# A graph attention layer on one core: more row loads on ACT, a new order of SP's loads at the end

## The chip, the cores and the metric

The kernel runs on one core of one Trainium2 chip. The core has five engines with a queue of their own: PE (matrix products), DVE and ACT (vector and scalar work), POOL (here: it issues gathers), and SP (it only issues transfers). The metric is device time in microseconds (us), the median of several runs.

## The reference

12,500 nodes with 128 features each, and 412,500 edges sorted by destination, each with 64 features. One layer of graph attention with 4 heads of 32:

```python
h = jnp.maximum(_layernorm(x, axis=-1), 0.0)
h = (h @ W_node.T).reshape(num_nodes, H, HD)
e = (edge_features @ W_edge.T).reshape(num_edges, H, HD)
att = jnp.sum(jnp.concatenate([h[src], h[tgt], e], axis=-1) * a, axis=-1)
att = jnp.where(att > 0, att, 0.2 * att)
m = jnp.maximum(segment_max(att, tgt), 0.0)
ex = jnp.exp(att - m[tgt])
denom = segment_sum(ex, tgt) + (num_edges - deg)[:, None] * jnp.exp(-m)
out = x + segment_sum((ex / denom[tgt])[:, :, None] * h[src], tgt)
```

So for every edge one row of `h` has to be fetched by its source, weighted, and added to the row of its destination.

## The kernel before

A first stage computes a table in the chip's memory: one row of 144 floats (576 bytes) per node, with the four heads of `h`, ones for the sums, and each node's parts of the logits. A second small table, `near`, holds the destinations' part.

The edges are then cut into 461 chunks of 896, that is 7 tiles of 128 edges each; 7 chunks make a batch, 49 tiles, and there are 66 batches, 0 to 65 (the last has 6 chunks). A loop written out by hand runs over them. In iteration b:

- POOL issues the gathers of batch b+1 (`gather`, L648). One gather fetches the 128 rows of one tile. Ahead of a batch's gathers stands a small memset (`gate`, L643) that waits until the scatter of batch b-2 is done, since the rows' buffers `hs` form a ring of three.
- One or two tiles of a batch are not gathered but fetched row by row (`by_row`): SP and ACT each issue single loads of 576 bytes at addresses that they first read into registers, up to 32 at once (`row_by_row`, L670 the addresses, L674 the loads). `act_rows(b)` is how many of a batch's rows ACT issues; SP issues the rest. ACT issues batch b+2's rows in iteration b, in pieces: `MIDDLE` behind the copy of `spread`, `WHILE` behind a merge that has an output part after it, the rest at the iteration's end (`act_some`). SP issues rows of batch b+1: up to `FRONT` of them before the node logits of batch b+1, and the rest behind, at least `SPROWS` an iteration, the surplus going to batch b+2.
- SP also loads the node logits of batch b+1 from `near` into the one buffer `lw` (`load_near`, L590), which must wait until the choice of batch b has read it; the edge features `eft` (L582); and `pen_sb` (L696).
- DVE and ACT weigh batch b (`weigh`, `weigh_part`): DVE waits for the batch's rows (L689), adds the logits (L765), runs two scans (L775, L777); ACT takes the exponentials (L780); DVE multiplies the rows (L831), and PE scatters them into sums by destination (L838).
- ACT copies `lw` for batch b+1 (`spread`, L603), DVE chooses from it by predicated copies (`choose`, L607 to L620) and marks the destinations (`mark`, L733).
- Every second iteration, and in each of the last ones, DVE merges the sums of the batches into the accumulator `acc` (`merge`). It reads the columns' numbers into registers (`columns`, L865) after the copy of `here` (L899) and before the multiplication of L902, which waits for ACT's two exponentials (L895, L896).
- When enough is merged, a part of the output is finished (`finish`): the output of 98 tiles is made in 15 parts, 13 of 7 tiles and the last two of 4 and 3. ACT takes L992, DVE L994 to L999, PE 32 products (L1006), DVE adds in two steps (L1011), and SP stores.

In the last iterations the order differs: in iteration 64 batch 65 is chosen and marked before batch 64 is weighed, and batch 65 is weighed in two parts, the first over four of its seven rows of tiles.

The sizes that the change touches:

```python
FRONT = 64
ACTROWS = 112
MIDDLE = 16
WHILE = 32
EVERY = 4
```

Of the kernel before, what the change touches and what calls it, by code (L numbers as in the profile page):

```python
# [16 lines left out]
ENG = mybir.EngineType  # L17
# [6 lines left out]
H = 4  # L24
# [7 lines left out]
CB = 2 * SB - 1  # L32
NBT = -(-NCH // CB)
# [6 lines left out]
W = 32  # L40
# [3 lines left out]
NB = -(-N // P)  # L44
NQ = NB * (P // W)
GB = 7
XB = 9
LOOSE = 1
# [17 lines left out]
RL = 32  # L66
SPROWS = 112
FRONT = 64
ACTROWS = 112
MIDDLE = 16  # L70
WHILE = 32
EVERY = 4
HEADROWS = 32
EPS = 1e-5

# [15 lines left out]

def by_row(b):

    return (1 if b % EVERY == 0 or b == LOOSE + 1 else 2) if LOOSE < b < NBT else 0


def act_rows(b):

    return 0 if b <= LOOSE + 1 else MIDDLE if b == NBT - 1 else ACTROWS


def merges():
# [15 lines left out]
def parts():  # L118


    got, b0 = [], 0
    for n in [GB] * (NB // GB - 1) + [GB - GB // 2, GB // 2]:
        last = (b0 + n) * P + 2 * W
        b = next((b for _, b in merges() if chunk_of(b + 1) * CE * N >= last * E), NBT - 1)
        got.append((b0, n, b if b0 + n < NB else NBT - 1))
        b0 += n
    return got
# [11 lines left out]
def kernel(  # L139
# [12 lines left out]
    nc = tc.nc  # L152
# [87 lines left out]
    with (  # L240
# [275 lines left out]
        k = -2  # L516
# [146 lines left out]
    def row_by_row(s, engine, kind, n):  # L663

        last = s.left
        s.left = max(0, last - n)
        some = last - s.left
        while last > s.left:
            first = max(s.left, last - RL, (last - 1) // P * P)
            _, at = nc.values_load_multi_w_load_instructions(  # L670
                row_at[s.b - 2:s.b - 1, first:last], engines=[kind], min_val=0, max_val=(NB * P - 1) * WIDE,
                skip_runtime_bounds_check_because="a src is below N, and N at most NB * P")
            for i, v in enumerate(at, first):
                by_itself(engine.dma_start(s.hs[i % P:i % P + 1, i // P, :].bitcast(U8),  # L674
                                           table_b[ds(v, WIDE)].rearrange("(o c) -> o c", o=1)),
                          f"lone{s.b}", lone_sems, lone_done, s.b % ROWSEMS)
            last = first
        return n - some
# [184 lines left out]
    def columns(c, k):  # L863

        _, got = nc.values_load_multi_w_load_instructions(  # L865
            q0[0:1, c:c + k], engines=[ENG.DVE], min_val=0, max_val=NQ - 2,
            skip_runtime_bounds_check_because="a dst is at most N, so its column is at most N // W")
        return got

    def merge(c0, count, r, breaks=None):  # L870

        n = count if breaks is None else 2 * count
        step = n // count
        breaks = new[:, c0:c0 + n] if breaks is None else breaks.rearrange("p c k -> p (c k)")
        flat = (AW - 1) * (n + 1)
        ended = c0 + count == NCH
        up = ps.tile([P, BANKS * 512], F32, name="up")
        f = up[:, :flat].rearrange("p (d c) -> p d c", d=AW - 1)
        nc.vector.memset(f[:, :, 0], 0.0)
        m = r[:, AW - 1, 1:n + 1]  # L880
        run = work.tile([P, MC + 1], F32, name="run")
        nc.vector.tensor_copy(run[:, 0:1], carry_m)
        mc = work.tile([P, MC], F32, name="mc")
        nc.vector.tensor_scalar(mc[:, :n], m, 0.0, None, op0=OP.max)
        nc.vector.tensor_tensor_scan(run[:, 1:n + 1], breaks, mc[:, :n], run[:, 0:1],
                                     op0=OP.add, op1=OP.max)
        if not ended:
            nc.vector.tensor_copy(carry_m, run[:, n:n + 1])
        dif = work.tile([P, 2, MC], F32, name="dif")
        nc.vector.tensor_tensor(dif[:, 1, :n], m, run[:, 1:n + 1], op=OP.subtract)  # L890
        nc.vector.tensor_tensor(dif[:, 0, :n], run[:, 0:n], run[:, 1:n + 1], op=OP.subtract)
        nc.vector.tensor_tensor(dif[:, 0, :n], dif[:, 0, :n], breaks, op=OP.add)
        nc.vector.tensor_scalar(f[:, HD + 1, 1:n + 1], breaks, 1.0 / BIG, 1.0, op0=OP.mult, op1=OP.add)
        scale = up[:, 512:512 + MC]
        nc.scalar.activation(scale[:, :n], dif[:, 1, :n], AF.Exp)  # L895
        nc.scalar.activation(f[:, :HD + 1, 1:n + 1], dif[:, 0, None, :n].to_broadcast([P, HD + 1, n]), AF.Exp)  # L896
        nc.vector.tensor_copy(r[:, :AW - 1, 0], carry)
        here = here_ps[:, :count, :]
        nc.vector.tensor_copy(here, lastm[:, c0:c0 + count, :])  # L899
        got = columns(c0, min(CB, count))  # L900
        part = r[:, :HD + 1, 1:n + 1]
        nc.vector.tensor_tensor(part, part, scale[:, None, :n].to_broadcast([P, HD + 1, n]), op=OP.mult)  # L902
        val = work.tile([P, CE], F32, name="up")[:, :flat].rearrange("p (d c) -> p d c", d=AW - 1)
        nc.vector.tensor_tensor_scan(val.rearrange("p d c -> p (d c)"), f.rearrange("p d c -> p (d c)"),
                                     r[:, :AW - 1, :].rearrange("p d c -> p (d c)"), 0.0,
                                     op0=OP.mult, op1=OP.add)
        if not ended:
            nc.vector.tensor_copy(carry, val[:, :, n])
        put = up[:, :MC * 2 * AW].rearrange("p (c j d) -> p c j d", c=MC, j=2)
        nc.vector.tensor_tensor(put[:, :count, :, AW - 1], here,  # L910
                                run[:, step:n + 1:step, None].to_broadcast([P, count, 2]), op=OP.mult)
        for k in range(2):
            nc.vector.tensor_tensor(put[:, :count, k, :AW - 1], val[:, :, step:n + 1:step].rearrange("p d c -> p c d"),
                                    here[:, :, k:k + 1].to_broadcast([P, count, AW - 1]), op=OP.mult)
        for i0 in range(0, count, CB):
            if i0:
                got = columns(c0 + i0, min(CB, count - i0))
            for i, v in enumerate(got):
                cols = acc[:, ds(v, 2), :]
                nc.vector.tensor_tensor(cols, cols, put[:, i0 + i, :, :], op=OP.add)  # L920
# [62 lines left out]
    def finish(pool, psum, tag, em, b0, n):  # L983

        q = slice(b0 * 4, (b0 + n) * 4)
        full = min(n, (N - b0 * P) // P)
        left = N - (b0 + full) * P
        xg = held_x.pop(b0, None)
        if xg is None:
            xg = load_part(pool, b0, n)  # L990
        em = em[:, :n * 4]
        nc.scalar.activation(em, acc[:, q, AW - 1], AF.Exp, scale=-1.0)  # L992
        rest = pool.tile([P, GB * 4], F32, name="rest")[:, :n * 4]
        nc.vector.tensor_scalar(rest, acc[:, q, HD + 1], -1.0, float(E), op0=OP.mult, op1=OP.add)  # L994
        nc.vector.tensor_tensor(em, em, rest, op=OP.mult)
        nc.vector.tensor_tensor(em, em, acc[:, q, HD], op=OP.add)
        nc.vector.reciprocal(em, em)
        wgt = pool.tile([P, BUF], F32, name="a")[:, :GB * 4 * HD].rearrange("p (q d) -> p q d", d=HD)
        nc.vector.tensor_tensor(wgt[:, :n * 4, :], acc[:, q, :HD], em[:, :, None].to_broadcast([P, n * 4, HD]),  # L999
                                op=OP.mult)  # L1000
        w4 = wgt.rearrange("p (b s) d -> p b s d", s=4)

        po = psum.tile([P, 2, 512], F32, name=tag)[:, :, :2 * GB * HD].rearrange("p k (h b d) -> p k h b d", h=2, d=HD)
        for h in range(H):
            for s in range(4):
                nc.tensor.matmul(po[s * W:(s + 1) * W, h // 2, h % 2, :n, :],  # L1006
                                 ident[:, h * W:(h + 1) * W], w4[:, :n, s, :], start=True, stop=True,
                                 tile_position=(0, s * W))
        for k in range(2):
            cols = xg[:, :n, k * 2 * HD:(k + 1) * 2 * HD].rearrange("p b (h d) -> p h b d", d=HD)  # L1010
            nc.vector.tensor_tensor(cols, po[:, k, :, :n, :], cols, op=OP.add)  # L1011

        def store():
            nc.sync.dma_start(out[b0 * P:(b0 + full) * P, :].rearrange("(b p) d -> p b d", p=P), xg[:, :full, :])
            if full < n:
                nc.scalar.dma_start(out[(b0 + full) * P:N, :], xg[:left, full, :])

        return store
# [76 lines left out]
    with tc.manual_schedule():  # L1095
# [17 lines left out]
        for b in range(NBT - 1):  # L1113
# [5 lines left out]
                batch(b + 3).ends = index(b + 3)  # L1119
            front = 0  # L1120
            if b:
                front = FRONT - row_by_row(batch(b + 1), nc.sync, ENG.SP, FRONT if b < NBT - 2 else FRONT // 2)
            load_near(batch(b + 1))
            if before and merge_of(b - 1)[1] == b - 1:
                for b0, n, behind in parts():
# [332 lines left out]
```

## Time and profile before

| | |
|---|---|
| median of 3 runs | 3956.34 us (3948.43 to 3957.4) |
| the profiled execution | 3947.4 us |
| its span, from the first to the last instruction | 3945.6 us |
| busy: POOL, DVE, PE, ACT | 75%, 62%, 28%, 11% |
| gathers issued by POOL (L648) | 3045 |
| row loads issued by SP, by ACT (L674) | 7248, 6960 |
| granted TensorE clock, mean | 0.603 |

Busy time counts an engine's own work; what a queue does to issue a transfer isn't counted, except that POOL's gathers are. In rows of the profile SPq and ACTq are the queues of SP and ACT, "x32" is a count of instructions merged into one row, and "[0.30 <-issue]" is idle time before an instruction and what ended it; "issue" means that no wait shows.

### The profile page before, as it was taken

The page shows a single profiled execution, that of the slowest core. Times are in us where ns is not written, and L with a number is a line of the kernel's source. Part 1 is how long each engine was busy: PE and PEld are TensorE (multiplying, and loading weights), DVE is VectorE, ACT ScalarE, POOL GpSimd, SP SyncE. Part 2 cuts the span into 40 slices and gives each one's busy share as a digit, 9 for nine tenths or more (in the row PEclk, how much of TensorE's full clock was granted, in tenths as well). Part 3 has the DMA queues.
Part 4 walks back from the last instruction along what each step waited for, and adds up shares of the span by engine and source line. Part 5 has one row for each costly group of instructions (what it writes and reads, how often), then busy time and mean ns, then how long its engine had stood idle before and what let it go on. Part 6 is the DMA issues. An engine that isn't in the chain of part 4 may idle for free.

```text
span 3945.6 us, 96319 instructions
## 1 busy us (share of the span) xinstructions
PE 1111.9 (28%) x27848; PEld 636.6 (16%) x27848; DVE 2452.5 (62%) x4384; ACT 433.4 (11%) x693; POOL 2952.7 (75%) x3188
## 2 busy tenths in 40 slices
PE   5532233223222232222222222232232222222231
PEld 4321011111111111111111111111111111011011
DVE  7766576556566566465566565566566566556577
ACT  5220011100110011011011010011011011011010
POOL 7777777777777777777777777777777777777773
PEclk9766666555665665565655665655555565656665
DMA  7444444444444444434444444434434434444431
GB/s 222 135 111 122 102 116 112 116 94 133 97 117 115 95 113 122 110 90 117 102 102 115 105 104 115 115 89 122 110 95 117 110 93 112 114 96 115 115 94 48
DMA packets 294926, 436.70 MB, mean 111 GB/s; under 512 B 84002, under 2 KB 207454, under 8 KB 294386
## 3 DMA queue, kind: packets, MB, share of 16 engines
q0 software_dynamic: 99584, 229.07, 26.0%
q1 hardware_dynamic: 167376, 189.90, 15.5%
q10 hardware_dynamic: 27426, 11.50, 1.3%
q8 instruction: 220, 3.60, 0.4%
q14 instruction: 320, 2.62, 0.2%
HBM read 414.67 MB, written 15.51 MB: 109 GB/s over the span
## 4 chain that ended last, share of the span: by engine, by line
POOL 48%; issue 20%; DVE 8%; SPq 7%; ACTq 7%; DMA 2%; PE 1%; ACT 1%; DVEq 0%; POOLq 0%
POOL hs L648 48%; ACTq L674 6%; SPq L674 5%; DVE hs L831 2%; DVE pick L620 1%; SPq L670 1%; ACTq L670 1%; DMA hs<-table,ends 1%; DMA lw<-near 1%; SPq L590 1%; DVE hot L733 1%; PE pa L838 0%; DVE up L775 0%; PE up L1006 0%; DVE m L777 0%
## 5 line engine op out<-in xcount | busy, mean ns | idle before, releaser
L648 POOL DMA_INDIRECT hs<-table,ends x3045 | 2880.0, 946 | 924.1 <-issue 921.6
L838 PE MATMUL pa<-hs,hot 128*32 128x35 f32 x25480 | 483.5, 243 | 2532.5 <-DVE hs L831 2164.3
L838 PEld LDWEIGHTS pa<-hs,hot 128*32 128x32 f32 x25480 | 426.6, 149 | 2625.1 <-issue 2533.2
L765 DVE TENSOR_TENSOR logits<-hs,pick 128x196 f32<-128x196 f32 x65 | 32.4, 498 | 878.6 <-DVEq L689 877.3
L714 PE MATMUL z<-eft,wa 128*32 128x512 f32 (+3 forms) x1056 | 493.0, 607 | 20.5 <-DMA eft<-in_ef 17.0
L831 DVE TENSOR_TENSOR hs<-hs,exr 128x924 f32<-128x924 f32 (+2 forms) x466 | 478.5, 1097 | 0.0
L780 ACT ACTIVATE both<-a 32x224 f32<-32x224 f32 (+2 forms) x268 | 103.2, 385 | 2801.3 <-DVE a L778 2067.3
L620 DVE COPY_PREDICATED pick<-exr,lw 128x3136 f32<-128x3136 int32 x65 | 237.5, 3654 | 11.5 <-ACT pick L603 9.8
L620 DVE COPY_PREDICATED pick<-exr,pick 128x1568 f32<-128x1568 int32 (+2 forms) x195 | 227.2, 1165 | 6.7
L603 ACT COPY pick<-lw 128x3136 f32<-128x3136 f32 x65 | 182.2, 2803 | 105.1 <-ACTq L689 88.6
L714 PEld LDWEIGHTS z<-eft,wa 128*32 128x32 f32 (+1 forms) x1056 | 106.9, 120 | 370.6 <-issue 359.3
L786 DVE STREAM_TRANSPOSE exr<-both 128x224 f32<-128x224 f32 (+1 forms) x67 | 28.3, 423 | 214.4 <-ACT both L780 212.7
L775 DVE TENSOR_TENSOR_SCAN up<-pen_sb,z 32x896 f32<-32x896 f32 (+1 forms) x67 | 133.3, 1990 | 34.7 <-DMA pen_sb<-pens 32.5
L920 DVE TENSOR_TENSOR acc<-acc,up 128x70 f32 x461 | 105.1, 228 | 67.2 <-issue 51.3
L777 DVE TENSOR_TENSOR_SCAN m<-pen_sb,up 32x896 f32<-32x896 f32 (+1 forms) x67 | 132.6, 1979 | 2.3
L733 DVE TENSOR_TENSOR hot<-exr,key 128x448 f32<-128x448 f32 (+1 forms) x260 | 128.9, 558 | 5.8
L770 DVE TENSOR_TENSOR up<-z,zst 32x224 f32<-32x224 f32 (+2 forms) x268 | 103.3, 385 | 13.0 <-PE z L714 0.2
L784 DVE SCALAR_TENSOR_TENSOR both<-pen_sb,up 32x224 f32<-32x224 f32 (+2 forms) x268 | 100.0, 373 | 3.8
L1006 PE MATMUL up<-a,ident 128*32 128x224 f32 (+2 forms) x480 | 44.5, 546 | 187.7 <-DVE a L999 187.7
L252 POOL DMA_INDIRECT hs<-in_x,ends x67 | 63.5, 948 | 20.4 <-issue 19.5
L774 DVE TENSOR_TENSOR z<-up,a 32x896 f32<-32x896 f32 (+1 forms) x67 | 72.0, 1075 | 2.3
L778 DVE TENSOR_TENSOR a<-z,m 32x896 f32<-32x896 f32 (+1 forms) x67 | 71.4, 1066 | 2.3
(192 smaller groups left out, 1102.6 us busy)
## 6 DMA issues: line engine op xcount, KB each, us to landing
eft<-in_ef SPq DMA_DIRECT2D x66, 1792.0 KB
hs<-table SPq DMA_DIRECT2D x7248, 0.6 KB
hs<-table ACTq DMA_DIRECT2D x6960, 0.6 KB
hs<-table,ends POOLq DMA_INDIRECT x3045
lw<-near SPq DMA_DIRECT2D x461, 64.0 KB
pen_sb<-pens SPq DMA_DIRECT2D x66, 98.1 KB
table<-rows ACTq DMA_DIRECT2D x9, 648.0 KB
xg<-in_x SPq DMA_DIRECT2D x13, 448.0 KB
```

The costliest lines, as they stand in the source:

```text
L603: nc.scalar.copy(s.pick[:, :, :s.chunks, :], lw[:, None, :s.chunks, :n].to_broadcast([P, T, s.chunks, n]))
L620: nc.vector.copy_predicated(s.pick[:, :, :s.chunks, :n], bit[:, :, :, None].to_broadcast([P, T, s.chunks, n]), more)
L648: load = nc.gpsimd.indirect_dma_start(out=s.hs[:n, t * CB + q, :], out_offset=None, in_=table[:, :], in_offset=bass.IndirectOffsetOnAxis(a ...
L674: by_itself(engine.dma_start(s.hs[i % P:i % P + 1, i // P, :].bitcast(U8), table_b[ds(v, WIDE)].rearrange("(o c) -> o c", o=1)), f"lone{s. ...
L714: s.made = own_half(s, nc.tensor.matmul(s.z[:, part], wa3[:n, j, :], s.eft[:n, j, part], start=(j == 0), stop=(j == SB - 1)))
L733: nc.vector.tensor_tensor(s.hot[:, :, q0:q0 + n, :].rearrange("p t q r -> p q t r"), rows_ps[:, None, None, :].to_broadcast([P, n, T, W]), ...
L770: on_half(s, nc.vector.tensor_tensor(grouped(up, g), grouped(s.z, g), zst[g * R:(g + 1) * R, t0:t1, :], op=OP.add))
L775: on_half(s, nc.vector.tensor_tensor_scan(up[:, e0:e1], s.pen[:, e0:e1], z, 0.0, op0=OP.add, op1=OP.max))
L777: nc.vector.tensor_tensor_scan(mp[:, ::-1], s.pen[:, e1:e0:-1], up[:, e0:e1][:, ::-1], 0.0, op0=OP.add, op1=OP.max)
L831: nc.vector.tensor_tensor(rows, rows, ex_ps[:, t0:t1, q * H:(q + 1) * H, None].to_broadcast([P, t1 - t0, H, HB]), op=OP.mult)
L838: scattered[s.b] = nc.tensor.matmul(pa[h * W:(h + 1) * W, q * AW:(q + 1) * AW], s.hot[:, t, q, :], s.hs[:, t * CB + q, h * AW:(h + 1) * AW ...
L920: nc.vector.tensor_tensor(cols, cols, put[:, i0 + i, :, :], op=OP.add)
```

## The change

ACT issues 128 rows of a batch instead of 112, and only one batch in eight (not in four) has a single tile by rows, so 118 tiles come by rows instead of 111. The last batch has one tile by rows (before: two), all by SP; of batch 64's rows ACT issues 80. In iterations 63 and 64 SP issues 96 and 48 rows ahead of the node logits (before: up to 64 and 32). The column numbers of a merge are loaded at its head. An output part's products are issued by halves, with DVE's addition of a half behind each. Of the last two output parts the first now has 3 tiles and the second 4.

```diff
-ACTROWS = 112
+ACTROWS = 128
-EVERY = 4
+EVERY = 8
 def by_row(b):
-    return (1 if b % EVERY == 0 or b == LOOSE + 1 else 2) if LOOSE < b < NBT else 0
+    if b in (LOOSE + 1, NBT - 1):
+        return 1
+    return (1 if b % EVERY == EVERY // 2 else 2) if LOOSE < b < NBT else 0
 def act_rows(b):
-    return 0 if b <= LOOSE + 1 else MIDDLE if b == NBT - 1 else ACTROWS
+    return 0 if b <= LOOSE + 1 or b == NBT - 1 else MIDDLE + 2 * WHILE if b == NBT - 2 else ACTROWS
 def parts():
-    for n in [GB] * (NB // GB - 1) + [GB - GB // 2, GB // 2]:
+    for n in [GB] * (NB // GB - 1) + [GB // 2, GB - GB // 2]:
 def merge(c0, count, r, breaks=None):
         breaks = new[:, c0:c0 + n] if breaks is None else breaks.rearrange("p c k -> p (c k)")
+        got = columns(c0, min(CB, count))
...
         nc.vector.tensor_copy(here, lastm[:, c0:c0 + count, :])
-        got = columns(c0, min(CB, count))
 def finish(pool, psum, tag, em, b0, n):
-        for h in range(H):
-            for s in range(4):
-                nc.tensor.matmul(po[s * W:(s + 1) * W, h // 2, h % 2, :n, :],
-                                 ident[:, h * W:(h + 1) * W], w4[:, :n, s, :], start=True, stop=True,
-                                 tile_position=(0, s * W))
         for k in range(2):
+            for h in (2 * k, 2 * k + 1):
+                for s in range(4):
+                    nc.tensor.matmul(po[s * W:(s + 1) * W, k, h % 2, :n, :],
+                                     ident[:, h * W:(h + 1) * W], w4[:, :n, s, :], start=True, stop=True,
+                                     tile_position=(0, s * W))
             cols = xg[:, :n, k * 2 * HD:(k + 1) * 2 * HD].rearrange("p b (h d) -> p h b d", d=HD)
             nc.vector.tensor_tensor(cols, po[:, k, :, :n, :], cols, op=OP.add)
 # the loop over batches
-                front = FRONT - row_by_row(batch(b + 1), nc.sync, ENG.SP, FRONT if b < NBT - 2 else FRONT // 2)
+                front = FRONT - row_by_row(batch(b + 1), nc.sync, ENG.SP, (MIDDLE + WHILE if b == NBT - 2 else FRONT + WHILE if b == NBT - 3 else FRONT))
```

## The prediction

> **What bounds the kernel now.** I read the page first, for the busy engine and the chain that ended last, then the waits, then the timeline of ACT, SP and POOL in three places: just after the start, in the middle, at the end.
>
> ```profile
> PE 1111.9 (28%) x27848; PEld 636.6 (16%) x27848; DVE 2452.5 (62%) x4384; ACT 433.4 (11%) x693; POOL 2952.7 (75%) x3188
> DMA  7444444444444444434444444434434434444431
> POOL 48%; issue 20%; DVE 8%; SPq 7%; ACTq 7%; DMA 2%; PE 1%; ACT 1%; DVEq 0%; POOLq 0%
> L648 POOL DMA_INDIRECT hs<-table,ends x3045 | 2880.0, 946 | 924.1 <-issue 921.6
> ```
>
> POOL issues 3045 gathers, 946 ns busy each and then 0.30 us in which it waits for nothing the profile shows: (2880.0 + 924.1) / 3045 = 1.249 us a gather, 3804 of the 3945.6 us. A batch has 49 tiles, of which 1 or 2 come row by row; 47 gathers are 58.7 us. So a tile taken off POOL is worth 1.249 us, as long as the rest keeps up. The waits show who keeps up:
>
> ```profile
> ACT both L780 <- DVE a L778: 2067.3, 48, 59.2
> ACT both L780 <- issue: 677.5, 17, 46.8
> SPq L590 <- DVE pick L620: 272.7, 20, 26.9
> DVE r L902 <- ACT up L896: 46.0, 34, 7.5
> DVE xg L1011 <- PE up L1006: 45.8, 14, 3.4
> ```
>
> The exponentials of L780 come once a batch, and behind them stand the multiplication and the scatter. In 48 cases ACT waited for DVE: there it had time to spare. In 17 it was released by "issue": DVE was ready and ACT's queue was still issuing row loads. ACT's 11% busy says nothing of this, for a row load is not counted as busy.
>
> **Step 1, POOL.** Tiles by rows go from 111 to 118: batches 8, 16, ... 64 get a second tile (8 gathers fewer), batch 65 loses one (1 more). 7 × 1.249 = 8.7 us off POOL's stream; 10.0 us off before batch 65's gathers begin.
>
> **Step 2, ACT issues 16 rows more a batch.** Does it fit? The middle of the run, ACT's timeline:
>
> ```profile
> 1506.34 1.58 ACT L780 ACTIVATE both<-a 32x224 f32<-32x224 f32 x4 [55.36 <-DVE a L778]
> 1523.04 10.53 ACTq L674 DMA_DIRECT2D hs<-table  x32
> 1535.06 26.09 ACTq L674 DMA_DIRECT2D hs<-table  x64
> 1563.90 1.59 ACT L780 ACTIVATE both<-a 32x224 f32<-32x224 f32 x4 [30.06 <-DVE a L778]
> 1623.71 1.59 ACT L780 ACTIVATE both<-a 32x224 f32<-32x224 f32 x4 [55.12 <-DVE a L778]
> 1640.05 37.70 ACTq L674 DMA_DIRECT2D hs<-table  x96
> 1683.26 1.59 ACT L780 ACTIVATE both<-a 32x224 f32<-32x224 f32 x4 [44.98 <-DVE a L778]
> 1685.60 45.77 ACTq L674 DMA_DIRECT2D hs<-table  x111
> 1741.72 1.59 ACT L780 ACTIVATE both<-a 32x224 f32<-32x224 f32 x4 [53.78 <-DVE a L778]
> ```
>
> From the exponentials to its last row ACT needs 54.8 us in a batch with a merge and an output part (1506.34 to 1561.15), 54.0 in one with a merge, 48.1 without: 102.5 us for two batches. Sixteen more rows cost 5.3 us by the 32 rows in 10.53 (which hold no load of offsets), 6.6 by the 111 in 45.77 (which hold four), 6.3 by the 96 in 37.70; I take 6.3, since the new pieces need about as many loads a row. That makes 115.1 us a pair, with 0.2 us between last row and next exponentials 115.3; the ends are 113.3 and 115.9. POOL's pair becomes 94.25 gathers and two gates, 117.9 us. ACT still fits, with 2.6 us to spare where it had 15. Where a merge batch has only 2.7 us free (1561.15 to 1563.90) the next exponentials come some 4 us late; the batch after it, with 10 us free, takes that up.
>
> But the run does not start level:
>
> ```profile
> 245.90 0.11 POOL L643 MEMSET gate<- 128x1 f32 x1
> 292.75 0.25 PE L838 MATMUL pa<-hs,hot 128*32 128x35 f32 x1
> 305.86 0.11 POOL L643 MEMSET gate<- 128x1 f32 x1
> 328.93 1.58 ACT L780 ACTIVATE both<-a 32x224 f32<-32x224 f32 x4 [39.77 <-issue]
> 1547.88 0.11 POOL L643 MEMSET gate<- 128x1 f32 x1
> ```
>
> The memset before each batch's gathers marks when the batch before it is issued. Batch 25 is issued at 1547.88 and has its exponentials at 1563.90, 16 us later; batch 3 is issued at 245.90 and has them at 328.93, 83 us later. ACT and DVE start 67 us behind POOL and have caught up by the middle. After the change this backlog is 67 + 2 × 6.3 = 80 us at batch 3 and shrinks by 2.6 us a pair instead of 15: 80 / 2.6 = 31 pairs, batch 65. It is used up only just before the end. On the way POOL itself must not stall: it may overwrite a buffer when the scatter of three batches before is done, 293.00 for the gate at 305.86, 12.9 us free. One batch of 6.3 us leaves 6.6. After that the room grew by 15 us a pair and now grows by 2.6, so it stays near 7 us for long. I cost a stall at nothing; if it comes, it is the few us by which 7 is exceeded, once.
>
> **Step 3, the end.** SP's order sets when batch 65's node logits (`lw`) are there.
>
> ```profile
> 1544.95 3.35 SPq L590 DMA_DIRECT2D lw<-near  x7
> 1550.19 18.22 SPq L674 DMA_DIRECT2D hs<-table  x48
> 1573.74 23.55 SPq L674 DMA_DIRECT2D hs<-table  x64
> 1598.71 3.50 SPq L590 DMA_DIRECT2D lw<-near  x7
> 1652.26 3.28 SPq L590 DMA_DIRECT2D lw<-near  x7
> 1658.40 36.00 SPq L674 DMA_DIRECT2D hs<-table  x96
> 1698.23 17.37 SPq L674 DMA_DIRECT2D hs<-table  x48
> 1717.00 3.34 SPq L590 DMA_DIRECT2D lw<-near  x7
> 3553.79 3.22 SPq L590 DMA_DIRECT2D lw<-near  x7
> ```
>
> From one load of node logits to the next SP needs 53.8 us with 112 rows between (1544.95 to 1598.71), 64.7 with 144. The line through both gives 59.2 for 128, 70.2 for 160, 48.3 for 96; simple proportion to 64.7 gives 57.5, 71.9 and 43.2. Batch 60's load (3553.79) waits for the choice of batch 59, not for SP, so it moves with POOL to 3545. By the new order 128 rows follow before batch 61's, 128 before 62's, 128 before 63's, 160 before 64's (96 now stand ahead of it) and 96 before 65's: 288 to 296 us. Batch 65's load is issued at 3833 to 3841, say 3838. Now the end as it is:
>
> ```profile
> 3811.75 1.55 DVE L784 SCALAR_TENSOR_TENSOR both<-pen_sb,up 32x224 f32<-32x224 f32 x4
> 3822.04 1.58 ACT L780 ACTIVATE both<-a 32x224 f32<-32x224 f32 x4 [26.04 <-issue]
> 3849.82 2.74 SPq L590 DMA_DIRECT2D lw<-near  x6
> 3852.84 0.12 POOL L643 MEMSET gate<- 128x1 f32 x1
> 3853.49 0.15 DVE L607 TENSOR_TENSOR away<-ends,floor 128x49 int32<-128x49 int32 x1
> 3856.11 2.43 ACT L603 COPY hs<-lw 128x2688 f32<-128x2688 f32 x1 [8.75 <-ACTq L689]
> 3867.38 0.49 DVE L765 TENSOR_TENSOR logits<-hs,pick 128x196 f32<-128x196 f32 x1
> 3904.10 0.33 DVE L765 TENSOR_TENSOR logits<-hs 128x96 f32<-128x96 f32 x1 [0.21 <-DVEq L689]
> ```
>
> Batch 64 is issued at 3852.84 and could be weighed some 6 us later (the last batch's 36 gathers end at 3897.8 by the pitch, and its weighing at 3904.10 found its rows there but for 0.21 us). It is weighed at 3867.38, because batch 65 is chosen and marked first and its node logits come late: load 3849.82, copy 3856.11, weighing 3867.38, 17.6 us from the first to the last. The whole tail hangs on this: 78.2 us from 3867.38 to the span's end. With the load at 3838 the weighing starts at 3855.6, 11.8 us earlier (8.5 to 16.8 by the ends for the load). Two things could hold it: batch 64's rows, there at 3852.84 - 10.0 + 6 = 3849, and DVE, free for batch 65's choice at 3853.49. DVE's work before that follows the exponentials of batch 63 by 31.5 us. These came 10.3 us after DVE was ready (3811.75), ACT still issuing 64 rows; now 32 rows stand there, so they come at 3811.7 - 8.7 = 3803 and DVE is free at 3834.5. The choice needs `lw` copied, 8.7 us after the load, at 3846.7: a backlog of up to 12 us is absorbed here.
>
> **Step 4, the small edits.** In the two merges of the tail, the column numbers now load ahead of the wait for ACT. DVE's idle there is 46.0 / 34 = 1.35 us a merge, mostly ACT's two exponentials; the change can gain at most 0.7 of it, or lose up to as much if DVE's queue stands still at the merge's head; hidden by the wait for the last sums, I take 0.35 each. Output by halves lets DVE's first addition run beside TensorE's second half: 45.8 / 14 = 3.3 us of waiting for 7 tiles, so 0.2 to 0.4 us in each of the two tail parts of 3 and 4 tiles; the swap of their sizes moves under 0.5 us from the last to the one before. 1.2 us together, 0 to 2; elsewhere POOL's stream covers them.
>
> **Sum.** 11.8 + 1.2 = 13.0 us. POOL's 8.7 isn't added: it permits the earlier tail. The span goes from 3945.6 to 3932.6, the profiled execution from 3947.4 to 3934.4; it lies 8.9 us below the median of 3956.34, which goes to 3943.3.
>
> **Rivals.** (A) *ACT's backlog is not used up.* If 16 rows cost more than 6.3 us, batch 63 starts its exponentials late, DVE is free later, and the tail moves with it. Each 0.1 us a pair is 3 us at the end, over 29.5 pairs. The gain is gone when 25 us are left (12 absorbed and 13 gained), at a pair of 116.0 (6.65 us for 16 rows): 80 - 29.5 × 1.9 = 24. At 117.0 53 us are left and it is 28 us slower, 3984; at 117.9 nothing is recovered and it is 55 us slower. For it: the 17 exponentials already released by "issue", and 6.6 us as my upper price. Against it: the price comes from equal pieces of the same run, and SP's steadier order (128 rows between node logits, not up to 144) removes waits of ACT in the first third. (B) *The tail isn't moved by SP's order*, because 96 rows ahead of batch 64's node logits only shift the delay to batch 65's, or DVE is late: then only POOL's 8.7 remain, or less: 3947 to 3953. (C) *Nothing moves*: row loads and gathers share the DMA engines, and a tile costs the same by either way; 3956. The DMA row above speaks against it, 4 tenths busy where POOL's pitch is 1.249 us throughout. The Trainium skill states this rule (DMA: Bandwidth & Descriptors, section "Issuing engines are not separate DMA queues"): DMAs of all issuing engines run on the same 16 engines, and issuing from several saves only issue time, usually small beside the transfer. By it the gain would be about nothing; here the trace differs, for the issue time is the bound. (D) *More*: SP reaches batch 65's load by 3832 and batch 64 is weighed as its rows land, at 3849: 19.6 us faster, 3937.
>
> **Chances.** A difference of 0.3%, 11.9 us, is about what a measurement of this kernel tells from none. Forecast 0.58, of which 0.41 over that bound and 0.17 within; A 0.24, of which 0.22 slower; B 0.10; C 0.04; D 0.04. So faster 0.45, same 0.33, slower 0.22. The forecast's own range is 3938 to 3948. To hold 8 in 10 the range takes in B and C and the nearer half of A: 3935 to 3974.
>
> **What would show it.** Right: 3038 gathers at 1.249 us; ACT's exponentials released by "issue" in most batches up to about 60; batch 65's node logits issued near 3838 and the weighing of batch 64 near 3855; batch 63's exponentials without ACT's delay; 78 us or a little less from there to the end. Wrong: exponentials released by "issue" through the last batches with the weighing of batch 64 after 3867 (A); idle time of POOL before a gate (a stall I cost at nothing); batch 65's load after 3845 (B).

## The result, and the profile after

The changed kernel takes 3973.12 us (median of ten runs, 3963.88 to 3980.71) against 3954.79 us of the kernel before in the same comparison: ratio 1.0047, 95% interval 1.0036 to 1.0059. That is 18.3 us slower; the forecast was 13.0 us faster. The profiled execution took 3980.7 us (span 3978.9), the slowest of the ten, and is 33.3 us longer than the profiled one of before. In some of the groups of runs below the kernel before took 7030 to 7060 us instead of 3955 (what is known of it stands at the end), so each number there stands beside its own kernel before.

The page of the changed kernel (busy time, chain, costliest groups). Line numbers are 2 to 3 higher than before: L650 are the gathers, L645 the gate, L782 the exponentials, L676 the row loads, L592 the node logits, L605 their copy, L767 the weighing, L979 the load of node features for an output part.

```profile
PE 1118.6 (28%) x27848; PEld 627.4 (16%) x27848; DVE 2454.8 (62%) x4384; ACT 431.6 (11%) x693; POOL 2955.0 (74%) x3181
ACTq 65%; issue 14%; DVE 12%; ACT 3%; DVEq 1%; SPq 0%; PE 0%; DMA 0%
L650 POOL DMA_INDIRECT hs<-table,ends x3038 | 2882.3, 949 | 923.2 <-issue 919.1
```

The chain that ended last was POOL's for 48%; now 65% of it is ACT's queue and POOL isn't named at all. Busy times hardly differ: a row load isn't counted as busy. The waits name the same thing (engine, line, what it waited for: us in total, times, longest):

```profile
ACT both L782 <- issue: 2791.5, 61, 52.4
ACT both L782 <- DVE a L780: 83.8, 6, 18.9
```

ACT's exponentials wait for ACT's own queue in 61 batches; before, in 17, and in 48 for DVE. ACT's timeline in the middle of the run:

```profile
1450.78 1.59 ACT L782 ACTIVATE both<-a 32x224 f32<-32x224 f32 x4 [50.57 <-issue]
1467.11 44.27 ACTq L676 DMA_DIRECT2D hs<-table  x112
1511.43 1.59 ACT L782 ACTIVATE both<-a 32x224 f32<-32x224 f32 x4 [46.07 <-issue]
1513.76 52.30 ACTq L676 DMA_DIRECT2D hs<-table  x127
1566.17 1.58 ACT L782 ACTIVATE both<-a 32x224 f32<-32x224 f32 x4 [50.06 <-issue]
1683.01 1.59 ACT L782 ACTIVATE both<-a 32x224 f32<-32x224 f32 x4 [51.19 <-issue]
```

In both batches shown with their row loads the last row ends within 0.15 us of the next exponentials (1513.76 + 52.30 = 1566.06, then 1566.17): ACT has nothing to spare. Two batches are 115.4 us (1450.78 to 1566.17), the next two 116.8 (to 1683.01). Over the whole run, the gates of batches 4 and 63, which mark when batches 3 and 62 are issued, and the exponentials of batches 3, 4 and 62:

```profile
247.35 0.12 POOL L645 MEMSET gate<- 128x1 f32 x1
343.81 1.59 ACT L782 ACTIVATE both<-a 32x224 f32<-32x224 f32 x4 [46.24 <-issue]
398.88 1.58 ACT L782 ACTIVATE both<-a 32x224 f32<-32x224 f32 x4 [50.39 <-issue]
3735.21 0.11 POOL L645 MEMSET gate<- 128x1 f32 x1
3777.76 1.58 ACT L782 ACTIVATE both<-a 32x224 f32<-32x224 f32 x4 [50.97 <-issue]
```

Batch 3's exponentials come 96.5 us after its issue, 80.5 more than the 16 us of a kernel without backlog: the forecast's 80. Batch 62's still come 42.6 us after its issue (18.1 before: gate 3733.91, exponentials 3752.03). ACT's mean pair is (3777.76 - 398.88) / 29 = 116.5 us. In between the delay falls slowly: from issue to exponentials it is 76 us at batch 24 and 57 us at batch 44. The tail starts with 25 us of ACT's backlog in it (42.6 less 18.1). None of POOL's 63 gates shows a wait. The tail, from SP's queue (node logits of batch 60, of 64, the load of node features, node logits of 65), ACT (exponentials of 63, copy for 65), POOL (gate of 65) and DVE (weighing of 64):

```profile
3581.92 3.26 SPq L592 DMA_DIRECT2D lw<-near  x7
...
3838.74 3.22 SPq L592 DMA_DIRECT2D lw<-near  x7
...
3867.04 0.40 SPq L979 DMA_DIRECT2D xg<-in_x  x1
...
3888.30 2.74 SPq L592 DMA_DIRECT2D lw<-near  x6
```

```profile
3838.46 1.59 ACT L782 ACTIVATE both<-a 32x224 f32<-32x224 f32 x4 [14.92 <-DVE a L780]
3894.68 2.43 ACT L605 COPY hs<-lw 128x2688 f32<-128x2688 f32 x1 [26.18 <-ACTq L691]
3852.86 0.11 POOL L645 MEMSET gate<- 128x1 f32 x1
3905.89 0.49 DVE L767 TENSOR_TENSOR logits<-hs,pick 128x196 f32<-128x196 f32 x1
```

The 33.3 us of the two profiles lie in three pieces: batch 62's exponentials 25.7 us later (3752.03 to 3777.76); from there to the weighing of batch 64 128.1 us instead of 115.4, 12.8 more; from that to the end 73.0 instead of 78.2, 5.2 less: a part of the output, which DVE finished there between the weighings of batches 64 and 65 (36.7 us apart before, 30.3 now), has left the tail. This execution is the slowest of the ten, so the pieces add up to 33.3 us and not to the 18.3 of the medians.

### The profile page after: what moved, and what is told of

It reads as the page before. It is cut to its first block, busy times and chain, and to the rows that moved or that the text cites. A ratio compares the mean times of both kernels' runs of the same rounds, so it can differ in the third digit from the quotient of the medians.

```text
span 3978.9 us, 98115 instructions
## 1 busy us (share of the span) xinstructions
PE 1118.6 (28%) x27848; PEld 627.4 (16%) x27848; DVE 2454.8 (62%) x4384; ACT 431.6 (11%) x693; POOL 2955.0 (74%) x3181
## 4 chain that ended last, share of the span: by engine, by line
ACTq 65%; issue 14%; DVE 12%; ACT 3%; DVEq 1%; SPq 0%; PE 0%; DMA 0%
ACTq L676 52%; ACTq L672 13%; DVE hs L833 6%; ACT both L782 2%; DVE hot L735 1%; DVE pick L622 1%; DVEq L867 0%; ACT up L899 0%; DVE hs L792 0%; DVE exr L788 0%; DVE zst L790 0%; SPq L676 0%; DVE run L888 0%; PE pa L840 0%; DVE key L731 0%
## 5 line engine op out<-in xcount | busy, mean ns | idle before, releaser
L650 POOL DMA_INDIRECT hs<-table,ends x3038 | 2882.3, 949 | 923.2 <-issue 919.1
L782 ACT ACTIVATE both<-a 32x224 f32<-32x224 f32 (+2 forms) x268 | 103.1, 385 | 2877.6 <-issue 2791.5
L605 ACT COPY pick<-lw 128x3136 f32<-128x3136 f32 x65 | 182.1, 2802 | 8.0 <-ACTq L691 8.0
L775 DVE TENSOR_SCALAR a<-up 32x896 f32<-32x896 f32 (+1 forms) x67 | 71.3, 1064 | 2.3
```

The source lines that it names most:

```text
L605: nc.scalar.copy(s.pick[:, :, :s.chunks, :], lw[:, None, :s.chunks, :n].to_broadcast([P, T, s.chunks, n]))
L650: load = nc.gpsimd.indirect_dma_start(out=s.hs[:n, t * CB + q, :], out_offset=None, in_=table[:, :], in_offset=bass.IndirectOffsetOnAxis(a ...
L782: nc.scalar.activation(both[g * R:(g + 1) * R, 0, t0:t1, :], grouped(att, g), AF.Exp)
```

## The experiments

**Theory B.** ACT's 16 more rows a batch make its cycle about as long as POOL's, the backlog of the start is carried through the run, and the tail starts with what is left. **Rivals.** T (called S in the first expectations): the new order of SP's loads in the tail costs. R: the rows cost at once, in every batch or in the last ones alone, and nothing is carried; each expectation says in which form. E: the loss is made early, by stalls of POOL that nothing makes up; against it, the changed kernel's gates show no wait.

### Where SP and ACT set the pace

Four kernels, run together on a chip on which the kernel before took 7059.73 us. The tail alone is the changed kernel with 112 rows a batch by ACT and 111 tiles again; the last batches keep the change's rows (80 of batch 64's and none of batch 65's by ACT, and one tile of batch 65):

```diff
-ACTROWS = 128
+ACTROWS = 112
-EVERY = 8
+EVERY = 4
-    if b in (LOOSE + 1, NBT - 1):
+    if b in (LOOSE + 1, NBT - 5, NBT - 1):
         return 1
-    return (1 if b % EVERY == EVERY // 2 else 2) if LOOSE < b < NBT else 0
+    return (1 if b % EVERY == 0 and b < NBT - 6 else 2) if LOOSE < b < NBT else 0
```

> The end's new order, the column numbers, the halves and the parts' order as after the change; rows as before it (112 a batch by ACT, 111 tiles), with the single-tile batches 4, 8, ... 56, 61 and 65. Theory B (ACT's backlog): the loss came from the 16 rows, so without them batch 62 starts level and the new end gains 5 to 14 us on the kernel before: 3941 to 3950. Rival S (SP's order at the end costs by itself: 96 rows and a load of x ahead of batch 65's node logits): slower than before by 5 to 20 us, with batch 65's node logits later than 3850.

7073.79 us, ratio 1.0016 (1.0007 to 1.0025); again in a later group 1.0017.

The rows alone are the kernel before with ACTROWS = 128, EVERY = 8, the new `by_row`, and no rows of batch 65 by ACT:

> Only the rows of the change: 128 a batch by ACT, 118 tiles, the last batch with one tile; SP's order at the end, the column numbers, the halves and the parts as before. Theory B: a pair of batches takes ACT 116 to 117 us, about 25 us of the starting backlog are left at batch 62, and the end is 15 to 35 us later than before: 3970 to 3990. Rival S: the rows alone give POOL's 8.7 us, 3943 to 3950.

7219.76 us, 1.0223 (1.0209 to 1.0237). Two kernels give the changed kernel's rows back in some batches only (`relieved`: b < 24 for early; 44 to 57 for late):

```diff
-    return (1 if b % EVERY == EVERY // 2 else 2) if LOOSE < b < NBT else 0
+    return (1 if b % (4 if relieved(b) else EVERY) == (0 if relieved(b) else EVERY // 2) else 2) if LOOSE < b < NBT else 0
-    return 0 if b <= LOOSE + 1 or b == NBT - 1 else MIDDLE + 2 * WHILE if b == NBT - 2 else ACTROWS
+    return 0 if b <= LOOSE + 1 or b == NBT - 1 else MIDDLE + 2 * WHILE if b == NBT - 2 else ACTROWS - 16 if relieved(b) else ACTROWS
```

> The whole change, but the batches up to 23 keep 112 rows by ACT and one single-tile batch in four (116 tiles by rows). Theory B: the starting backlog is gone by batch 24, as it was in the kernel before by about batch 21; 128 rows then just fit, and the end is 8 to 18 us earlier than before: 3937 to 3947. Rival R (128 rows cost something in every batch, not only through the backlog): 42 of 62 batches still have them, so two thirds of the loss stay: 3960 to 3970. Rival S: 3965 to 3980.

> The whole change, but batches 44 to 57 keep 112 rows by ACT and one single-tile batch in four: the same 116 tiles by rows as with the early batches relieved, at the other end of the run. Theory B: what is left of the backlog at batch 44 (some 45 us) is used up within four pairs, so the time is that of the early relief within 5 us: 3937 to 3950. A rival by which the harm is done at the start (POOL stalling at its gates while ACT is far behind): no gain, 3965 to 3980. Rival R: 48 batches still have 128 rows, 3962 to 3972.

Early relief 1.0168 (1.0153 to 1.0182; in three more groups 1.0193, 1.0181 and 1.0171), late relief 1.0185 (1.0171 to 1.0199; again 1.0189). None of these is in its expected range, for POOL does not set the pace here. The waits of the rows alone, and its queues around one pause of POOL (no gathers from 2018 to 2064):

```profile
POOL gate L645 <- PE pa L840: 3098.6, 63, 73.8
...
ACT both L782 <- issue: 5644.2, 62, 102.8
```

```profile
2042.29 18.35 SPq L676 DMA_DIRECT2D hs<-table  x48
2062.95 39.73 ACTq L676 DMA_DIRECT2D hs<-table  x31
2064.34 46.09 SPq L676 DMA_DIRECT2D hs<-table  x27
```

While POOL waits at its gate a row takes SP 0.38 us; while it gathers, 1.3 us on ACT and 1.7 on SP. So SP and ACT bound every batch, POOL waits 49 us at each gate, and a backlog cannot be carried. There 128 rows cost 160.0 us in 62 batches, 2.6 us a batch; the early kernel's 124.6 us less the tail's 14.1 are 2.8 for each of its 40 batches with 128 rows, the late one's 2.5 for each of 47. Each batch pays its share at once, as rival R has it, and the rows, not the tail's order, carry nine tenths of these two kernels' loss. Whether a backlog is carried where POOL sets the pace these runs could not say.

Fewer rows than before, 96 by ACT, with 103 tiles by rows (the single tiles where b % 8 is 0, 3 or 6):

> The kernel after with 96 rows a batch by ACT and 103 tiles by rows (15 fewer), the order of the tail, the columns, the halves and the parts as after. Theory B (the price of the change is ACT's issuing): on a chip where the kernel before takes about 3955 us ACT has 30 us a pair to spare and POOL bounds the kernel, with 8 gathers more than before: 10 us slower than before, less 5 to 10 us from the tail, 3955 to 3965 us, ratio 0.999 to 1.003. On a chip where the kernel before takes about 7060 us, where SP and ACT bound it through the whole run, 16 rows fewer a batch give 2.6 us a batch: 6900 to 6930 us, ratio 0.976 to 0.982. Theory S (there SP, not ACT, is the bound, and its rows are the same): 7040 to 7080 us there, ratio 0.997 to 1.003.

7030.99 us against 7056.87, 0.9965 (0.9951 to 0.9979): 26 us gained, between the two theories and much nearer to S. ACT's exponentials still waited for "issue" in 42 batches, and SP had the same 7248 rows. With fewer than 112 rows by ACT, then, SP seems to be most of the limit there; which of the two queues it is in a batch was not followed.

### What slows the queues there

All tiles gathered, no row loads (`by_row` and `act_rows` return 0); and the same with 220 copies a batch by ACT in place of its rows:

```diff
-            row_by_row(batch(b), nc.scalar, ENG.Activation, n)
+            for _ in range(n):
+                nc.scalar.copy(idle[:, 1:], idle[:, :1].to_broadcast([P, LONG - 1]))
```

> The kernel after without any row loads by SP and ACT: all 49 tiles of every batch are gathered by POOL. On the chips of these experiments a row load of SP or ACT took 1.4 us instead of 0.32 us in about 60 us of each batch, and these 60 us are the time of POOL's 47 gathers. Theory W (the row loads are slowed by POOL's gathers beside them, and nothing else of the kernel is slower here): without row loads POOL bounds the kernel: 3156 gathers at 1.249 us and 140 us around them, 4060 to 4130 us, ratio 0.575 to 0.585, and no wait of POOL before a gate. Theory V (these chips are slower whatever is issued): 5500 us or more.

> The kernel without row loads, in which ACT makes 220 copies of 23 numbers in each batch from 3 to 64 (28 of them behind the copy of the node logits, up to 56 behind a merge with an output part, the rest at the iteration's end), in the places where it issued row loads; they keep ACT busy and change nothing else. At about 0.2 us a copy that is 44 us a batch, and with exponentials, copies and merges about 105 us a pair, against 122.8 us of POOL for 98 gathers and two gates. Theory B (ACT costs time only by a backlog that is left at the end): no difference to the kernel without row loads, within 15 us. Rival R (each delay of the exponentials is paid at once): 200 us or more above it.

Without rows the kernel took 5266.41 us (0.7461, 0.7447 to 0.7474), so both theories on it missed; with the copies it took 7100.92 us, in a single execution, far above what either theory on them meant. The first expectation blamed the row loads alone. In the kernel without them PE's weight loads wait 1764 times for nothing that the profile shows ("issue"; 308 times in the kernel before at 3947 us), and POOL waits at its gates for PE:

```profile
PEld pa L838 <- issue: 3767.4, 1764, 32.3
...
POOL gate L643 <- PE pa L838: 1024.9, 63, 75.7
```

The copies wait mostly for the copy before. In ACT's timeline POOL issues gathers until 3045.3 and then none until 3091:

```profile
ACT idle L690 <- ACT idle L690: 2462.6, 2590, 1.5
```

```profile
3042.72 0.21 ACT L690 COPY idle<-idle 128x23 f32<-128x23 f32 x1 [1.19 <-ACT idle L690]
3053.22 18.76 ACT L690 COPY idle<-idle 128x23 f32<-128x23 f32 x78 [0.49 <-ACT idle L690]
```

Beside the gathers a copy of 0.21 us comes every 1.40 us; from 8 us after the last gather on 78 copies take 18.76 us, 0.24 us each. In the kernel without rows PE's products for the scatter come every 2.80 us beside the gathers, and 155 of them in 2.55 us in a pause of POOL (at 3033.63). So ACT and PE are slowed beside POOL's gathers there even without a row load: the row loads' own transfers are not the cause. What it is in the gathers that slows them isn't shown. As both kernels lacked a POOL that sets the pace, they say nothing on the backlog.

### Room for the rows

The kernel before, and the rows alone, with POOL made slower; this pair ran where the kernel before took 3956.97 us:

```diff
+PADS = 22
...
+            for _ in range(PADS):
+                nc.gpsimd.memset(s.hs[:, by_row(s.b):CB * EARLY, :], 0.0)
         for t, q in s.tiles:
```

> The kernel before, in which POOL also clears 26 of a batch's 49 rows of tiles 22 times ahead of the batch's gathers (about 3.2 us each, 71 us a batch; the gathers overwrite what is cleared). POOL then needs 58.8 + 71 = 130 us a batch, more than the 105 us in which SP and ACT issued their rows on these chips, so that POOL sets the pace again as it did at 3955 us: 63 batches of 130 us and about 350 us around them, 8450 to 8650 us, and no wait of POOL before a gate. This is the base for the next run.

> The same 22 clearings, and ACT's 128 rows with 118 tiles by rows (the kernel before otherwise). Theory B (16 more rows a batch cost only where ACT's cycle is longer than POOL's, or as long as its backlog isn't used up): with 20 us of room a batch the rows are free and the 7 gathers that POOL saves remain: 2 to 15 us less than the padded kernel before. Rival R (the rows cost by themselves, through the transfer engines or the supply of instructions, whoever sets the pace): about 160 us more than the padded kernel before, as without padding.

8514.03 and 8485.88 us: with 128 rows 28.2 us less. The clearings, one group of each page (first the padded kernel before, then with 128 rows), account for part of it:

```profile
L648 POOL MEMSET hs<- 128x3744 f32 (+1 forms) x1386 | 4504.3, 3250 | 76.4
```

```profile
L650 POOL MEMSET hs<- 128x3744 f32 (+1 forms) x1386 | 4485.9, 3237 | 76.4
```

That is 18.4 us, because a tile by rows isn't cleared, which the expectation had overlooked; 7 gathers of 1.249 us are 8.7 more, together 27.1. ACT's exponentials, in the waits of the kernel with 128 rows, wait for DVE in 65 batches, and for ACT's own queue in only 2:

```profile
ACT both L785 <- DVE a L783: 7278.4, 65, 130.1
```

With room, 16 rows a batch are free and POOL's gathers are saved, as step 1 and step 2 have it. R is out in the form that the rows cost by themselves, whoever sets the pace; whether a delay is carried this pair doesn't tell, since there is none.

### The backlog where POOL sets the pace

The early kernel and the tail alone once more, each where the kernel before took 3950 us:

> The kernel after with 112 rows a batch by ACT and a single tile every fourth batch in the batches before 24 only (116 tiles by rows). Where the kernel before takes about 3956 us: theory B (ACT's backlog is carried from batch to batch, so relief anywhere is relief at the end): about 10 pairs of 102.5 us against 118 us of POOL use up the backlog before batch 24, and later pairs of 116.5 us stay under POOL's 117.9; batch 62's exponentials come 16 to 20 us after its gate time instead of 42.6: 3937 to 3952 us, faster than before. Rival R (a batch's delay is local, and only the last batches count) and rival T (the order of the tail is what costs): like the kernel after, 3965 to 3980 us, slower than before. Where the kernel before takes about 7050 us: a ratio of 1.017 as measured already.

3945.23 us against 3950.64, ratio 0.9986 (0.9977 to 0.9995). It has the changed kernel's tail and its 128 rows in every batch from 24 on (80 in batch 64, as there), and is faster than before where the changed kernel is slower: the rows of 21 early batches decide. Its waits, and the gate and exponentials for batch 62:

```profile
ACT both L787 <- DVE a L785: 1450.5, 34, 56.9
ACT both L787 <- issue: 1049.7, 25, 46.3
```

```profile
3732.88 0.12 POOL L650 MEMSET gate<- 128x1 f32 x1
3752.86 1.59 ACT L787 ACTIVATE both<-a 32x224 f32<-32x224 f32 x4 [53.11 <-DVE a L785]
```

20.0 us and a wait for DVE, not 42.6 and "issue". Theory B is shown, and T and both forms of R fall with one run: rows that cost in every batch would have left two thirds of the loss. Late relief was not run where POOL sets the pace.

> The kernel after with ACT's rows, the single tiles and the 111 tiles by rows of the kernel before; the order of the tail, the columns, the halves and the parts as after. Where the kernel before takes about 3956 us: theory B (the price is ACT's rows alone): the tail's edits bring 5 us by the part that leaves the tail and up to 9 by SP's order, since no backlog is left: 10 us or less faster than before, ratio 0.996 to 1.000; as the kernel with relief in the early batches (0.9986) saves 5 gathers more, its ratio should stand 6 us or 0.15% above that one's if POOL's gathers are what counts. Rival T (the order of the tail is what costs): ratio 1.003 to 1.008. Where the kernel before takes about 7050 us: 1.0017 as measured already.

3942.77 us against 3950.04, 0.9982 (0.9973 to 0.9991): T falls a second time, the tail's edits are a gain of 7 us. But the last clause missed: with 5 gathers more than early relief it is not slower. SP's queue and DVE show why, first with early relief (node logits of 60, load of node features, rows, node logits of 65; then the weighings of 64 and 65), then the node logits of 65 and the weighing of 64 with the tail alone:

```profile
3551.26 3.33 SPq L597 DMA_DIRECT2D lw<-near  x7
...
3834.46 0.40 SPq L984 DMA_DIRECT2D xg<-in_x  x1
3837.20 17.38 SPq L681 DMA_DIRECT2D hs<-table  x48
3855.77 2.74 SPq L597 DMA_DIRECT2D lw<-near  x6
```

```profile
3873.50 0.49 DVE L772 TENSOR_TENSOR logits<-hs,pick 128x196 f32<-128x196 f32 x1
3904.51 0.32 DVE L772 TENSOR_TENSOR logits<-hs 128x96 f32<-128x96 f32 x1 [0.21 <-DVEq L696]
```

```profile
3849.28 2.74 SPq L592 DMA_DIRECT2D lw<-near  x6
3867.45 0.48 DVE L767 TENSOR_TENSOR logits<-hs,pick 128x196 f32<-128x196 f32 x1
```

With early relief batch 65's node logits are loaded at 3855.77, 6 us later than with the tail alone and than before the change, though POOL issued batch 64 2.5 us earlier (gate 3850.36 against 3852.84). SP's order, as the change has it, did not bring the tail forward even without a backlog. Hence a last edit to the early kernel:

```diff
-    return 0 if b <= LOOSE + 1 or b == NBT - 1 else MIDDLE + 2 * WHILE if b == NBT - 2 else ...
+    return 0 if b <= LOOSE + 1 else MIDDLE if b == NBT - 1 else MIDDLE + 2 * WHILE if b == NBT - 2 else ...
-..., (MIDDLE + WHILE if b == NBT - 2 else FRONT + WHILE if b == NBT - 3 else FRONT))
+..., (0 if b == NBT - 2 else FRONT + WHILE if b == NBT - 3 else FRONT))
```

> The kernel with relief in the batches before 24, with one more edit: SP issues no rows of batch 65 ahead of that batch's node logits (48 there before), and ACT issues 16 of its 128 rows. The prediction's step 3 says that the tail hangs on this load. In the kernel with early relief it stood at 3855.8 us in SP's queue, batch 64 was weighed at 3873, batch 65 at 3904.5, though POOL's gathers would have let it be weighed at about 3894 (the gate at 3850.4 and 43.3 us, as in the kernel with the tail alone). Theory L (the load is the limit of the tail): it goes to about 3838, batch 64 is weighed near 3857, batch 65 near 3894, where its gathers are the limit; 10 us less than with early relief alone, ratio 0.995 to 0.997. Rival M (batch 65's own rows, now issued behind the load, or DVE, are as late): ratio 0.998 to 1.000. Where the kernel before takes about 7050 us: 1.015 to 1.018.

This ran where the kernel before took 7038.44 us: ratio 1.0112 (1.0095 to 1.0129), less than early relief's 1.017 to 1.019 there and below the 1.015 expected. Once more:

> The kernel with relief in the batches before 24, with one more edit: SP issues no rows of batch 65 ahead of that batch's node logits (48 there before), and ACT issues 16 of its 128 rows. Where the kernel before takes about 3950 us: theory L (the load of batch 65's node logits is the limit of the tail): it goes from 3855.8 us to about 3838, batch 64 is weighed near 3857 (3873 with early relief alone), batch 65 near 3894 (3904.5), where its gathers are the limit; 10 us less than with early relief alone, ratio 0.995 to 0.997. Rival M (batch 65's own rows, now issued behind the load, or DVE, are as late): ratio 0.998 to 1.000. Where the kernel before takes about 7050 us: 1.011 as measured already.

3939.36 us against 3957.46: 0.9953 (0.9940 to 0.9967), 18 us faster than before, so that it beats both kernels. Against early relief it is 6 us less by the two times and 13 by the two ratios, for the kernel before differs by 7 us between the two groups. Its chain, SP's queue, the gate of 65 and the weighings:

```profile
POOL 70%; issue 23%; DVE 4%; PE 1%; DMA 1%; ACTq 0%; ACT 0%; POOLq 0%; DVEq 0%
```

```profile
3836.50 0.40 SPq L984 DMA_DIRECT2D xg<-in_x  x1
3838.08 2.74 SPq L597 DMA_DIRECT2D lw<-near  x6
```

```profile
3854.46 0.12 POOL L650 MEMSET gate<- 128x1 f32 x1
3860.81 0.49 DVE L772 TENSOR_TENSOR logits<-hs,pick 128x196 f32<-128x196 f32 x1
3892.70 0.33 DVE L772 TENSOR_TENSOR logits<-hs 128x96 f32<-128x96 f32 x1 [0.21 <-DVEq L696]
```

Theory L holds: the load at 3838.08, batch 64 weighed 6.4 us after its issue, and the chain is POOL's for 70%, where it was 45% with early relief and ACT's queue for 65% in the changed kernel. That batch 65's gathers limit its weighing isn't shown: it follows batch 64's by 31 to 32 us here, with early relief and with the tail alone, though the gate stands 6.4, 23.1 and 12.2 us ahead of batch 64's. How the 18 us divide between this load, POOL's 5 gathers and the part that left the tail was not measured one by one.

## Why the prediction was wrong

The forecast (faster) failed and rival A happened, with a piece that the prediction had ruled out. The median of 3973.12 us lies inside the wide range, 3935 to 3974, only because that range takes in the nearer half of A; the forecast's own range was 3938 to 3948. By its steps:

- **Step 1, POOL: the count right, the gain not there.** 3038 gathers, and none of POOL's stalls at a gate. But (2882.3 + 923.2) / 3038 = 1.253 us a gather, not 1.249, and batch 65's gate came at 3852.86, where 10.0 us less than 3852.84 were forecast. The same group with early relief and in the last kernel, which issue the same rows:

```profile
L655 POOL DMA_INDIRECT hs<-table,ends x3040 | 2877.4, 947 | 925.4 <-issue 921.9
```

```profile
L655 POOL DMA_INDIRECT hs<-table,ends x3040 | 2883.2, 948 | 923.9 <-issue 922.7
```

1.251 and 1.252 us. So equal kernels in this respect differ by 0.1%, and the five profiles of unpadded kernels at this pace span 0.3%, 10 us over the run: as much as the step was worth.
- **Step 2, ACT's price: the term that was mis-sized.** 6.3 us for 16 rows made a pair of 115.3 us; the pair measured 116.5. A batch without a merge takes 54.6 us from its exponentials to its last row (1511.43 to 1566.06) where it took 48.1, 6.5 us more in that batch and 6.9 on average over the pairs ((116.5 - 0.2 - 102.5) / 2, the 0.2 us being those between last row and exponentials). So 25 us of backlog were left where none was forecast. By A's rule 116.5 would leave 39; that it was 25 is mostly because POOL was slower too, a pair of 118.2 us by the gates (3735.21 - 247.35 over 29.5 pairs) where 117.9 was forecast. The upper bound, 6.6, was nearer; a pair lay above the upper end, 115.9, too. The start was right (80.5 us of backlog for 80), and so was the warning that each 0.1 us a pair is 3 us at the end: "used up only just before the end" had no margin at all, and this should have weighed more than 0.24.
- **Step 3, the absorbed 12 us: false.** Step 3 let SP's chain run free of ACT: "batch 60's load waits for the choice of batch 59, not for SP, so it moves with POOL to 3545". The choice of batch 59 stands on DVE behind the multiplication, merge and output part that follow batch 58's exponentials: these came at 3543.04 and the choice at 3578.15, before the change at 3515.54 and 3550.03. So the load carries ACT's backlog: it came at 3581.92, and every later load with it. DVE, forecast to be free for batch 65's choice at 3834.5, came to it at 3873.31, and the node logits only at 3888.30: nothing was there to absorb the backlog. With 25 us left A's rule gave no gain and no loss; the kernel lost 18.
- **Step 3, SP's span: too short.** From batch 60's load to 65's 288 to 296 us were forecast; with 128 rows by ACT it took 306.4 in the changed kernel and 304.5 with early relief (3551.26 to 3855.77). One term was left out, the load of node features: the part of 3 tiles is now finished in iteration 63, so its load stands ahead of batch 65's node logits and waits for a store; SP issued it at 3867.04 behind a store of 3863.33. With early relief that wait is 4.1 us, half of the 8.5 by which the span exceeds 296; the rest was not traced. So rival B would have come true had A not: with no backlog the tail gained nothing by SP's order. That the tail hangs on this load was right: once it did stand at 3838, by the last edit, batch 64 was weighed at 3860.8 (3855.6 forecast).
- **Step 4 and the tail's length: better than said.** From the weighing of batch 64 to the end 73.0 us, in the others 74, where 78.2 or a little less was forecast: nearly all of these 4 to 5 us come with the part of 3 tiles that is finished earlier, where "under 0.5" was forecast for the swap; what the column numbers and the halves add was not measured alone. Batch 63's exponentials came without a wait for ACT's rows, as forecast, but at 3838.46 and not at 3803, for DVE itself was late by then.
- **Rival C** is out in both directions: with room the tiles by rows save POOL's gathers, without it the rows cost. Its page, the Trainium skill's DMA: Bandwidth & Descriptors, section "Issuing engines are not separate DMA queues", holds issue time to be usually small beside the transfer. In this trace issue time decides: ACT's queue is 65% of the chain.

The padded pair, early relief and the tail alone show that the rows cost by ACT's backlog; the pieces of the tail are read from the traces. Why the pitch differs between executions stays open.

## What to carry to other kernels

When work is moved to a queue that has room, compare its cycle with the pace-setter's over the whole run, starting backlog included: a queue that is level in the middle may spend the whole run paying off its start, and a margin of 2% in the cycle is no margin. Here it paid to relieve the queue in the first batches, while the backlog is there, and to load it afterwards; relief late in the run was not measured at this pace. In a tail, follow each load back to what its queue has ahead of it, the output's loads too, before counting on an earlier engine.

## What the runs showed of the hardware

In 13 of 18 runs, on three chips, the kernel before took 7030 to 7062 us. There SP and ACT took 1.3 to 1.7 us for a row while POOL gathered and 0.38 us while it waited, and without row loads ACT's plain copies came every 1.40 us beside the gathers and every 0.24 us without; POOL's gathers stayed at 0.945 to 0.948 us. In the other groups a row took 0.3 to 0.4 us beside the gathers (127 in 52.30 us). What decides between the two was not found: one chip showed both, 3957 us in one group of runs and 7033 us in the next. Where the gathers slowed the other queues, the kernel without row loads was the fastest by far (5266 us); it was not run where POOL sets the pace.
